# Routers of three mixtures of experts: first choice from the logits, sums by one scan, one product for all ranks, and two parts a turn for one pair

## The chip, the cores and the metric

The kernel runs on 1 core of one Trainium2 chip. The metric is the device time of one execution in microseconds (us). The core has a matmul engine (TensorE, PE in the profile; PEld is its weight load), a vector engine (VectorE, DVE), a scalar engine (ScalarE, ACT), a general engine (GpSimd, POOL) and a queue for transfers (SyncE, SP). Each engine works through its own list of instructions in order and waits for the others by semaphores.

## What is computed

Four layers stand in a row, each as half a feed-forward part, an attention, and the same feed-forward part again. The input is 4 batches of 512 tokens of 128 numbers, all float32. The feed-forward parts of layers 0 and 3 are mixtures of experts with a capacity; only their routers are changed. Cut to what matters:

```python
# layer 0 (used twice): one choice, 8 experts, capacity 320
logits = einsum('td,ed->te', tokens, gate_w)
probs = softmax(logits)
mask = one_hot(argmax(probs), 8)
ranks = cumsum(mask, axis=0) - 1.0              # over all 2048 tokens
keep = (ranks < capacity) * mask
h = relu(einsum('ecd,edh->ech', dispatch, w1) + b1)
out = einsum('ech,ehd->ecd', h, w2) + b2
ans = combined out, weighted by probs

# layer 3 (used twice): two choices, 8 experts, capacity 512
scores = softmax(xt @ wg)
gates_k, idx_k = top_k(scores, 2)
gates_k = gates_k / sum(gates_k)
m = masks of first choices of all tokens, then of second choices
loc = cumsum(m) - 1 at each token's choice      # place within the expert
valid = loc < cap
# rows are placed at (expert, loc), run through the expert, gathered back,
# weighted by gates_k * valid
```

## The kernel before

Tokens lie on the 128 partitions: a batch is 4 tiles of 128 tokens (`NT = 4`), 16 tiles in all (`TILES`).

A `Mixture` object stands for one use of such a part: `f00` and `f01` are the two of layer 0 (`k = 1`), `f30` and `f31` the two of layer 3 (`k = 2`). Its method `tokens` is the router for one batch, or for two batches together as a pair (`G = 4` or `8` tiles). It normalizes the rows (`norms`: statistics on DVE, `rs`, a power for `rstd` and sometimes `off` on POOL, then the scaling on DVE, ACT or POOL), transposes them on PE, multiplies by the gate weights (`lg`, L322), takes a softmax, and finds the first choice (`route`, and for two choices `without` and `route` again). `masks` then holds ones at the chosen expert. `pre` is a running sum of the masks over the tiles of the call and of earlier calls (`cum`), by one DVE addition for each tile (L359). The rank of a token within its expert comes from two products on PE for each choice: `before` (ones where an earlier token of the tile stands) times the mask (L368), and `ones` times `pre` (L369). From the rank DVE computes `kept`, `at`, `slot`, `keep` and the row address `to` (L372 to L385). Last, POOL copies the weights `counts` into the rows (L392) and writes each tile of rows to its place in the DRAM buffer `disp` with an indirect transfer, here called a scatter (L395): one for each tile and choice.

`experts` reads `disp` back expert by expert (`d_f`, L426, issued from SP), so it starts only when the last scatter of the mixture has landed. It runs the two matrix products, and writes rows to `res` with scatters of its own (L489); `combine` adds them to the tokens.

The routers stand in four places:

- `f00` at the start of the kernel: four batches, staggered by two turns (`skewed`).
- `f01` beside the attention of layer 0: each batch's router starts when that batch's attention output is done, so the router of batch 3 runs after the attention's end. Transposes of the next weights (`prep_l1`, L137 to L140) follow.
- `f30` at the end of a chain of feed-forward parts of layers 1 and 2. Here the batches go in two pairs, (0, 1) and (2, 3). The pairs go through the same parts, the second pair 8 turns behind the first (`whole(skewed([behind(pool, bs) for bs in pairs], 8))`). The first pair uses one call of `tokens` with `later=4`, which lets four turns pass before the scatters; the second pair uses two calls, one for each batch, 3 turns apart.
- `f31` beside the attention of layer 3, as `f01`.

A turn is one step of the Python generators, from one `yield` to the next. It sets the order in which instructions are written down. In the attentions that order is kept for PE, DVE, ACT and POOL (`manual_schedule`). In the chain with `f30` it is kept for POOL alone. Everywhere else a planner at compile time sorts each engine's list by its own estimate of when operands are ready.

The POOL list of the chain, near its end, is therefore written by hand: the norms of the first pair's router, those of batch 2, those of batch 3, the first pair's 16 scatters, the 8 of batch 2 and the 8 of batch 3.

Of the kernel before, what the change touches and what calls it, by code (L numbers as in the profile page):

```python
# [41 lines left out]
def kernel(ctx: ExitStack, tc: tile.TileContext, a: dict, out: bass.AP):  # L42
# [25 lines left out]
    for b in range(NB):  # L68
# [12 lines left out]

    before = const([P, P], "before")
    nc.gpsimd.affine_select(
        out=before, in_=ones, pattern=[[1, P]], compare_op=ALU.is_gt, fill=0.0, base=0, channel_multiplier=-1
    )
    mhalf = const([P, 2 * NT], "mhalf")
    nc.gpsimd.memset(mhalf, -0.5)
# [113 lines left out]
    def bc_mid(ap, shape):  # L201
        return ap.unsqueeze(1).to_broadcast(shape)


    def route(pool, src, g, tag, mask=None):

        mx = pool.tile([P, g], FP, name=f"mx_{tag}", tag=f"mx_{tag}")
        nc.vector.tensor_reduce(mx, src, AX.X, ALU.max)
        eq = pool.tile([P, g, E], FP, name=f"eq_{tag}", tag=f"eq_{tag}")
        nc.vector.tensor_tensor(eq, src, bc(mx, [P, g, E]), ALU.is_equal)  # L210
        nc.vector.tensor_tensor(eq, eq, bc_mid(e_rank, [P, g, E]), ALU.mult)
        first = pool.tile([P, g], FP, name=f"first_{tag}", tag=f"first_{tag}")
        nc.vector.tensor_reduce(first, eq, AX.X, ALU.max)
        if mask is None:
            mask = pool.tile([P, g, E], FP, name=f"mask_{tag}", tag=f"mask_{tag}")
        nc.vector.tensor_tensor(mask, eq, bc(first, [P, g, E]), ALU.is_equal)
        return mask, mx

    def without(pool, src, mask, g, low, tag):
        rest = pool.tile([P, g, E], FP, name=f"rest_{tag}", tag=f"rest_{tag}")  # L220
        nc.vector.scalar_tensor_tensor(rest, mask, low, src, ALU.mult, ALU.add)
        return rest

    def softmax(pool, lg, g, tag):

        mx = pool.tile([P, g], FP, name=f"smx_{tag}", tag=f"smx_{tag}")
        nc.vector.tensor_reduce(mx, lg, AX.X, ALU.max)
        pr = pool.tile([P, g, E], FP, name=f"pr_{tag}", tag=f"pr_{tag}")
        nc.vector.tensor_tensor(pr, lg, bc(mx, [P, g, E]), ALU.subtract)
        nc.scalar.activation(pr, pr, AF.Exp)  # L230
        yield
        sm = pool.tile([P, g], FP, name=f"sm_{tag}", tag=f"sm_{tag}")
        nc.vector.tensor_reduce(sm, pr, AX.X, ALU.add)
        nc.vector.reciprocal(sm, sm)
        nc.vector.tensor_tensor(pr, pr, bc(sm, [P, g, E]), ALU.mult)
        return pr

# [3 lines left out]
    class Mixture:  # L241
# [7 lines left out]
        def __init__(self, tag, cap, k):  # L249
# [32 lines left out]

        def tokens(self, bs, wT, on="vector", pool=None, fine=False, later=0):

# [7 lines left out]
            for n, b in zip(ns, bs):  # L292
                for c in range(k):
# [43 lines left out]
            counts = tile("counts", [P, k, G])  # L337
            if k == 1:
                nc.vector.tensor_scalar(counts[:, 0], best, 0.5, None, ALU.mult)
            else:  # L340
                if fine:
                    yield
                rest = without(pool, pr, masks[:, 0], G, -4.0, f"r{G}")
                _, second = route(pool, rest, G, f"r1{G}", masks[:, 1])
                total = tile("total", [P, G])
                nc.vector.tensor_tensor(total, best, second, ALU.add)
                nc.vector.reciprocal(total, total)
                nc.vector.scalar_tensor_tensor(counts[:, 0], best, 0.5, total, ALU.mult, ALU.mult)
                nc.vector.scalar_tensor_tensor(counts[:, 1], second, 0.5, total, ALU.mult, ALU.mult)
            if fine:  # L350
                yield

            pre = routing.tile([P, k, G + 1, E], FP, name=f"pre_{tag}", tag=f"pre{k}{G}")
            if self.cum is None:
                nc.vector.memset(pre[:, :, 0, :], 0.0)
            else:
                nc.vector.tensor_copy(pre[:, :, 0, :], self.cum)
            for t in range(G):
                nc.vector.tensor_tensor(pre[:, :, t + 1, :], pre[:, :, t, :], masks[:, :, t, :], ALU.add)  # L359
            self.cum = pre[:, :, G, :]  # L360
            yield
            if fine:
                yield

            ps = bank(f"rank_{tag}")[:, : k * G * E].rearrange("p (k g e) -> p k g e", k=k, e=E)
            for c in range(k):
                out = ps[:, c].rearrange("p g e -> p (g e)")
                nc.tensor.matmul(out, before, masks[:, c].rearrange("p g e -> p (g e)"), start=True, stop=False)  # L368
                nc.tensor.matmul(out, ones, pre[:, c, :G, :].rearrange("p g e -> p (g e)"), start=False, stop=True)  # L369
            yield  # L370
            kept = tile("kept", [P, k, G, E])
            nc.vector.scalar_tensor_tensor(kept, ps, float(self.cap), masks, ALU.is_lt, ALU.mult)  # L372
            at = tile("at", [P, k, G, E])
            nc.vector.tensor_tensor(at[:, 0], ps[:, 0], bc_mid(first_row[self.per], [P, G, E]), ALU.add)
            if k == 2:
                nc.vector.tensor_tensor(at[:, 1], bc_mid(last_row, [P, G, E]), ps[:, 1], ALU.subtract)
            nc.vector.tensor_tensor(at, at, kept, ALU.mult)
            slot = tile("slot", [P, k, G])
            nc.vector.tensor_reduce(slot, at, AX.X, ALU.add)
# [3 lines left out]
            nc.vector.tensor_tensor(keep, keep, spare, ALU.mult)  # L383
            to = tile("to", [P, k, G], I32)
            nc.vector.tensor_tensor(to, slot, keep, ALU.subtract)  # L385
            yield

            for _ in range(later):
                yield
            for i, n in enumerate(ns):  # L390
                for c in range(k):
                    nc.gpsimd.tensor_copy(n[:, :, 1 if c else D + 3], counts[:, c, i * NT : (i + 1) * NT])  # L392
            for c in range(k):
                for t in range(G):
# [5 lines left out]
                    )  # L400
                    if fine and t % 2:
                        yield
# [1072 lines left out]
    with tc.tile_pool(name="weights12", bufs=1) as mid:  # L1475
# [15 lines left out]
        def behind(pool, bs):  # L1491
# [70 lines left out]
```

## Time and profile before

| | |
|---|---|
| median of 3 runs | 1575.8 us (1572.78 to 1575.96) |
| profiled execution | 1557.3 us, of which the span of the profile is 1555.6 us |
| mean granted PE clock | 0.898 of full speed |
| PE busy | 1279.9 us (82%), 10651 instructions |
| DVE busy | 866.6 us (56%), 2955 instructions |
| ACT busy | 713.2 us (46%), 1487 instructions |
| POOL busy | 657.2 us (42%), 791 instructions |
| scatters of the routers (L395) | 96, 94.6 us on POOL |
| additions of the running sums (L359) | 64 on DVE |
| rank products (L368 and L369) | 88 PE records (a float32 product shows as two) |

All profile numbers come from the profiled execution and are times in us from the start of its span. In a line of a timeline the first number is the start and the second the length, then engine, source line, operation, what is written and what is read with their shapes (partitions x elements), how many such instructions were merged (x), and in brackets the idle time of the engine before it and what ended that.

### The profile page before, as it was taken

What the parts mean: (1) busy time and instruction counts of PE and PEld (TensorE: products, weight loads), DVE (VectorE), ACT (ScalarE), POOL (GpSimd) and SP (SyncE); (2) the same over time, 40 slices, a digit from 0 to 9 for tenths busy, and PEclk for the clock granted to TensorE, in tenths of its full rate; (3) what the DMA queues carried; (4) which work ended last, traced back from release to release, by engine and by line L of the source; (5) the groups of instructions that cost most, each with busy time, mean ns of one, the idle gap of its engine ahead of it and who ended that gap; (6) DMA issues with size and microseconds to landing.
All of it is one profiled execution on the core that took longest, in us unless ns stands there. A gap on an engine that the chain in (4) does not pass through costs nothing. (4 is left out here: it accounts for less than half of the span.)

```text
span 1555.6 us, 28883 instructions
## 1 busy us (share of the span) xinstructions
PE 1279.9 (82%) x10651; PEld 823.0 (53%) x10651; DVE 866.6 (56%) x2955; ACT 713.2 (46%) x1487; POOL 657.2 (42%) x791
## 2 busy tenths in 40 slices
PE   3787998995969688989989887819789999998394
PEld 3464666773755455757656666606533334333273
DVE  5325776773335366666556556615367787773343
ACT  1234876871443156768743322203336655564041
POOL 3455767772420177677510111263631224212253
PEclk9897999996989988999989878858979999999597
DMA  7520230002415375442022000014204000000233
GB/s 226 129 57 13 77 146 32 9 6 65 140 49 111 94 219 150 140 133 70 2 56 55 1 0 1 10 61 103 62 21 172 15 5 12 13 3 15 76 79 105
DMA packets 100660, 106.21 MB, mean 68 GB/s; under 512 B 9084, under 2 KB 73832, under 8 KB 100520
## 3 DMA queue, kind: packets, MB, share of 16 engines
q1 hardware_dynamic: 93864, 91.16, 20.8%
q0 software_dynamic: 6656, 13.22, 2.6%
q8 instruction: 84, 1.38, 0.4%
q14 instruction: 56, 0.46, 0.1%
HBM read 62.49 MB, written 41.85 MB: 67 GB/s over the span
## 5 line engine op out<-in xcount | busy, mean ns | idle before, releaser
L605 POOL TENSOR_SCALAR sc_a<-sc_a,top_a 128x128 f32<-128x128 f32 (+3 forms) x256 | 276.0, 1093 | 110.6 <-DVE top_a L604 75.1
L587 PE MATMUL s_a<-k_a,q_a 32*128 32x512 f32 (+3 forms) x1536 | 266.5, 548 | 17.1 <-POOL k_a L1183 13.8
L692 ACT ACTIVATE w_a<-t_a 128x512 f32<-128x512 f32 x256 | 140.4, 595 | 119.6 <-PE t_a L587 94.9
L628 PE MATMUL t_a<-ident,sc_a 128*128 128x128 f32 x1280 | 172.3, 282 | 6.2 <-DVE top_a L608 5.7
L489 POOL DMA_INDIRECT res_f<-y_f,back_f x112 | 109.8, 980 | 143.7 <-ACT y_f L488 102.3
L587 PE MATMUL t_a<-ql_a,k_a 32*128 32x512 f32 x512 | 168.8, 644 | 0.5 <-DVE low_a__12755 L672 0.2
L628 PEld LDWEIGHTS t_a<-ident,sc_a 128*128 128x128 f32 x1280 | 145.2, 144 | 36.4 <-issue 13.7
L617 ACT ACTIVATE sc_a<-sc_a,top_a 128x128 f32<-128x128 f32 (+3 forms) x256 | 134.9, 577 | 22.8 <-DVE top_a L608 22.6
L587 PEld LDWEIGHTS s_a<-k_a,q_a 32*128 32x128 f32 x1536 | 93.7, 188 | 88.1 <-issue 42.8
L637 ACT ACTIVATE w_a<-t_a 128x256 f32<-128x256 f32 (+2 forms) x192 | 94.3, 526 | 63.6 <-PE t_a L628 63.1
L395 POOL DMA_INDIRECT disp_f<-n_f,to_f x96 | 94.6, 985 | 66.7 <-issue 58.8
L501 PE MATMUL o_f<-w_l,h_f 128*128 128x128 f32 (+1 forms) x896 | 113.0, 279 | 3.8 <-DVE o_f L483 3.3
L501 PEld LDWEIGHTS o_f<-w_l,h_f 128*128 128x128 f32 (+1 forms) x896 | 103.0, 184 | 14.7 <-DVE o_f L483 6.0
L466 PE MATMUL h_f<-dT_f,w_l 128*128 128x320 f32 (+1 forms) x256 | 108.0, 560 | 2.8 <-ACT dT_f L444 2.8
L157 POOL TENSOR_SCALAR rs_f<-mv_f 128x4 f32<-128x4 f32 (+1 forms) x23 | 5.7, 248 | 230.0 <-DVE mv_f L154 229.2
L650 PE MATMUL acc_a<-w_a,vpad 128*32 128x128 f32 x2560 | 98.4, 280 | 0.6 <-DVE top_a L604 0.6
L639 ACT COPY w_a<-t_a 128x256 f32<-128x256 f32 (+2 forms) x192 | 93.7, 527 | 6.9 <-PE t_a L628 6.6
L672 DVE TENSOR_REDUCE low_a__12755<-s_a 128x1 f32<-128x512 f32 x128 | 82.1, 685 | 26.3 <-PE t_a L587 18.5
L608 DVE CUSTOM_DVE_ANT_0 sc_a<-s_a,future 128x128 f32<-128x128 f32 (+3 forms) x128 | 62.3, 487 | 56.4 <-PE s_a L587 50.3
L672 DVE TENSOR_REDUCE low_a__12753<-s_a 128x1 f32<-128x512 f32 x128 | 81.3, 683 | 20.1 <-PE t_a L587 15.0
L608 DVE CUSTOM_DVE_ANT_0 sc_a<-s_a,table 128x128 f32<-128x128 f32 (+3 forms) x128 | 62.4, 488 | 52.9 <-PE s_a L587 52.4
L488 ACT ACTIVATE y_f<-o_f,d_f 128x128 f32<-128x128 f32 (+1 forms) x112 | 38.8, 394 | 105.9 <-DVE o_f L483 105.9
(343 smaller groups left out, 2285.9 us busy)
## 6 DMA issues: line engine op xcount, KB each, us to landing
fac_a<-fac_a_sb SPq DMA_DIRECT2D x36, 256.0 KB
disp_f<-zeros_f SPq DMA_DIRECT2D x4, 2080.0 KB
d_f<-disp_f SPq DMA_DIRECT2D x32, 260.0 KB
w_l<-in_L_ffn_w_dram SPq DMA_DIRECT2D x16, 512.0 KB
cb_f<-rows_f SPq DMA_DIRECT2D x16, 512.0 KB
q_a<-fac_a SPq DMA_DIRECT2D x32, 256.0 KB
k_a<-fac_a SPq DMA_DIRECT2D x32, 256.0 KB
r_f<-res_f SPq DMA_DIRECT2D x24, 256.0 KB
```

Of the source, the lines that this page charges most:

```text
L395: nc.gpsimd.indirect_dma_start(out=self.to[c][i0 + t][:, :], out_offset=bass.IndirectOffsetOnAxis(ap=to[:, c, t : t + 1], axis=0), in_=ns[ ...
L466: nc.tensor.matmul(ps[u][:, :cap], w1[:, e, (c + u) * P : (c + u + 1) * P], dT, start=True, stop=True)
L489: nc.gpsimd.indirect_dma_start(out=self.back[e * per + s][:, :], out_offset=bass.IndirectOffsetOnAxis(ap=back[:m, s : s + 1], axis=0), in_ ...
L501: nc.tensor.matmul(po[:m, s, :], h[:, c, s * P : s * P + m], w2[:, e, c, :], start=(c == 0), stop=(c == NC - 1),)
L587: nc.tensor.matmul(ps[:, n0:n1], q[r : r + SLOT, i * P : (i + 1) * P], k[r : r + SLOT, n0:n1], start=True, stop=True)
L605: nc.gpsimd.tensor_scalar(sc, sc, top, None, ALU.subtract)
L608: nc.vector.tensor_tensor_reduce(sc, banks[r][:, :n], more, -1.0, HUGE, ALU.add, ALU.min, top)
L617: nc.scalar.activation(sc, sc, AF.Exp, bias=top, scale=-1.0)
L628: nc.tensor.transpose(ps[:, x * n + j * P : x * n + (j + 1) * P], st["sc", u, i, r0 + x][:, j * P : (j + 1) * P], ident,)
L650: nc.tensor.matmul(st["acc", u][r * SLOT : (r + 1) * SLOT, i * P : (i + 1) * P], vpads[b % 2][:, j, g * 4 + r, :], st["w", u, i, r][:, j * ...
L672: nc.vector.tensor_reduce(st["low", u][:, i, c : c + 1], ps, AX.X, ALU.max, negate=True)
L692: nc.scalar.activation(w, ps, AF.Exp)
```

## The change

The router `tokens` is rewritten in these points:

- The first choice is taken from the logits in PSUM instead of from the softmax; `softmax` as a function is gone. The exponentials are still made, for the second choice and the weights. With one choice the weight is half the reciprocal of the sum of the exponentials; with two, the best has the value 1, so the sum is `second + 1`.
- `masks`, `pre`, `kept` and `at` are laid out with the tiles innermost (`[P, k, E, G]`).
- `pre` is made by one `tensor_tensor_scan`, a multiplication by `goes_on` (zero at the first tile of each expert, else one) and an addition. It is the sum within the call and includes the tile itself; what came before is kept apart in `cum`.
- The ranks of all choices come from one accumulated product: `not_before` (the old `before` minus one) times the masks, `ones` times `cum` spread over the tiles if there is one, and `ones` times `pre`.
- `spare` and the start row of each expert minus `spare` (`ends`) are made once for each mixture; `keep` is gone, and `to` is `slot + spare`.
- `later` is gone. The first pair's call of `f30` is made with `apart=True`, which yields after every scatter, and is advanced by two parts each turn.

```diff
+    nc.vector.tensor_scalar(not_before, not_before, -1.0, None, ALU.add)
+    goes_on = {}
+    for g in (NT, 2 * NT):
+        goes_on[g] = const([P, 2 * E * g], f"goes_on{g}")
+        nc.vector.memset(goes_on[g], 1.0)
+        nc.vector.memset(goes_on[g].rearrange("p (e t) -> p e t", t=g)[:, :, 0], 0.0)
...
-    def route(pool, src, g, tag, mask=None):
+    def route(pool, src, g, tag, mask=None, mx=None):
...
+            self.spare = routing.tile([P, TILES], FP, name=f"spare_{tag}", tag=f"spare{k}", bufs=1)
+            nc.vector.tensor_scalar(self.spare, tok_id[:, :TILES], float(self.rows), None, ALU.add)
+            self.ends = routing.tile([P, k, E, TILES], FP, name=f"ends_{tag}", tag=f"ends{k}", bufs=1)
+            for c, row in enumerate((first_row[self.per], last_row)[:k]):
+                nc.vector.tensor_tensor(
+                    self.ends[:, c], bc(row, [P, E, TILES]), bc_mid(self.spare, [P, E, TILES]), ALU.subtract
+                )
...
-            spare = pool.tile([P, k, G], FP, name=f"spare_{tag}", tag=f"spare{k}{G}")
-            nc.gpsimd.tensor_scalar(
-                spare, bc_mid(tok_id[:, i0 : i0 + G], [P, k, G]), float(self.rows), None, ALU.add
-            )
...
-            pr = yield from softmax(pool, plg[:, : G * E].rearrange("p (g e) -> p g e", e=E), G, f"r{G}")
-            masks = tile("masks", [P, k, G, E])
-            _, best = route(pool, pr, G, f"r0{G}", masks[:, 0])
...
+            nc.vector.tensor_reduce(mx, lg, AX.X, ALU.max)
+            pr = tile("pr", [P, G, E])
+            nc.vector.tensor_tensor(pr, lg, bc(mx, [P, G, E]), ALU.subtract)
+            nc.scalar.activation(pr, pr, AF.Exp)
+            masks = tile("masks", [P, k, E, G])
+            by_tile = [masks[:, c].rearrange("p e g -> p g e") for c in range(k)]
+            route(pool, lg, G, f"r0{G}", by_tile[0], mx)
+            yield
+            if k == 2:
+                rest = without(pool, pr, by_tile[0], G, -4.0, f"r{G}")
+                _, second = route(pool, rest, G, f"r1{G}", by_tile[1])
                 if fine:
                     yield
...
-            for t in range(G):
-                nc.vector.tensor_tensor(pre[:, :, t + 1, :], pre[:, :, t, :], masks[:, :, t, :], ALU.add)
-            self.cum = pre[:, :, G, :]
+            nc.vector.tensor_tensor_scan(
+                pre.rearrange("p k e g -> p (k e g)"), goes_on[G][:, : k * E * G],
+                masks.rearrange("p k e g -> p (k e g)"), 0.0, ALU.mult, ALU.add,
+            )
...
-            for c in range(k):
-                out = ps[:, c].rearrange("p g e -> p (g e)")
-                nc.tensor.matmul(out, before, masks[:, c].rearrange("p g e -> p (g e)"), start=True, stop=False)
-                nc.tensor.matmul(out, ones, pre[:, c, :G, :].rearrange("p g e -> p (g e)"), start=False, stop=True)
+            nc.tensor.matmul(ps, not_before, masks.rearrange("p k e g -> p (k e g)"), start=True, stop=False)
+            if self.cum is not None:
+                nc.tensor.matmul(
+                    ps.rearrange("p (e g) -> p e g", g=G), ones,
+                    bc(self.cum.rearrange("p k e -> p (k e)"), [P, k * E, G]), start=False, stop=False,
+                )
+            nc.tensor.matmul(ps, ones, pre.rearrange("p k e g -> p (k e g)"), start=False, stop=True)
+            counts = tile("counts", [P, k, G])
+            total = tile("total", [P, G])
+            if k == 1:
+                nc.vector.tensor_reduce(total, pr, AX.X, ALU.add)
+            else:
+                nc.vector.tensor_scalar(total, second, 1.0, None, ALU.add)
+            nc.vector.reciprocal(total, total)
+            nc.vector.tensor_scalar(counts[:, 0], total, 0.5, None, ALU.mult)
+            if k == 2:
+                nc.vector.tensor_tensor(counts[:, 1], second, counts[:, 0], ALU.mult)
+            cum = routing.tile([P, k, E], FP, name=f"cum_{tag}", tag=f"cum{k}")
+            if self.cum is None:
+                nc.vector.tensor_copy(cum, pre[:, :, :, G - 1])
+            else:
+                nc.vector.tensor_tensor(cum, self.cum, pre[:, :, :, G - 1], ALU.add)
+            self.cum = cum
...
-            keep = tile("keep", [P, k, G])
-            nc.vector.tensor_reduce(keep, kept, AX.X, ALU.add)
-            nc.vector.tensor_tensor(slot, slot, spare, ALU.add)
-            nc.vector.tensor_tensor(keep, keep, spare, ALU.mult)
+            nc.vector.tensor_reduce(slot, at.rearrange("p k e g -> p k g e"), AX.X, ALU.add)
             to = tile("to", [P, k, G], I32)
-            nc.vector.tensor_tensor(to, slot, keep, ALU.subtract)
+            nc.vector.tensor_tensor(to, slot, bc_mid(self.spare[:, i0 : i0 + G], [P, k, G]), ALU.add)
             yield
-            for _ in range(later):
-                yield
...
-                    if fine and t % 2:
+                    if apart or (fine and t % 2):
                         yield
...
             if bs[0] == 0:
-                yield from f30.tokens(bs, l3["gate"], "scalar", pool, later=4)
+                parts = f30.tokens(bs, l3["gate"], "scalar", pool, apart=True)
+                while next(parts, "end") != "end" and next(parts, "end") != "end":
+                    yield
```

More of the change, by code (lines that the diff above doesn't have):

```diff
@@ L80 @@
     )
-    before = const([P, P], "before")
+    not_before = const([P, P], "not_before")
     nc.gpsimd.affine_select(
-        out=before, in_=ones, pattern=[[1, P]], compare_op=ALU.is_gt, fill=0.0, base=0, channel_multiplier=-1
+        out=not_before, in_=ones, pattern=[[1, P]], compare_op=ALU.is_gt, fill=0.0, base=0, channel_multiplier=-1
     )
+    nc.vector.tensor_scalar(not_before, not_before, -1.0, None, ALU.add)
[4 more added lines that the diff above has]
+        nc.vector.memset(goes_on[g].rearrange("p (e t) -> p e t", t=g)[:, :, 0], 0.0)
     mhalf = const([P, 2 * NT], "mhalf")
@@ L202, in bc_mid @@
         return ap.unsqueeze(1).to_broadcast(shape)
-    def route(pool, src, g, tag, mask=None):
-        mx = pool.tile([P, g], FP, name=f"mx_{tag}", tag=f"mx_{tag}")
-        nc.vector.tensor_reduce(mx, src, AX.X, ALU.max)
+    def route(pool, src, g, tag, mask=None, mx=None):
+        if mx is None:
+            mx = pool.tile([P, g], FP, name=f"mx_{tag}", tag=f"mx_{tag}")
+            nc.vector.tensor_reduce(mx, src, AX.X, ALU.max)
         eq = pool.tile([P, g, E], FP, name=f"eq_{tag}", tag=f"eq_{tag}")
@@ L222, in without @@
         return rest
[L224 to L230, printed above, removed]
-        yield
[L232 to L236, printed above, removed]
     routing = ctx.enter_context(tc.tile_pool(name="routing", bufs=2))
@@ L281, in clear, with tokens @@
             self.spread_zeros(self.res[1 : 1 + self.k * T, :])
-        def tokens(self, bs, wT, on="vector", pool=None, fine=False, later=0):
+        def tokens(self, bs, wT, on="vector", pool=None, fine=False, apart=False):
             pool = pool or routing
@@ L333, in tokens @@
             yield
-            pr = yield from softmax(pool, plg[:, : G * E].rearrange("p (g e) -> p g e", e=E), G, f"r{G}")
-            masks = tile("masks", [P, k, G, E])
-            _, best = route(pool, pr, G, f"r0{G}", masks[:, 0])
[L337 to L340, printed above, removed]
+            lg = plg[:, : G * E].rearrange("p (g e) -> p g e", e=E)
+            mx = tile("mx", [P, G])
@@ L341, in tokens @@
                 if fine:
                     yield
[L343 to L357, printed above, removed]
-            for t in range(G):
-                nc.vector.tensor_tensor(pre[:, :, t + 1, :], pre[:, :, t, :], masks[:, :, t, :], ALU.add)
-            self.cum = pre[:, :, G, :]
+            pre = routing.tile([P, k, E, G], FP, name=f"pre_{tag}", tag=f"pre{k}{G}")
@@ L361, in tokens @@
+            nc.vector.tensor_tensor_scan(
+                pre.rearrange("p k e g -> p (k e g)"),
+                goes_on[G][:, : k * E * G],
+                masks.rearrange("p k e g -> p (k e g)"),
+                0.0, ALU.mult, ALU.add,
+            )
             yield
@@ L363, in tokens @@
                 yield
[L365 to L369 removed]
+            ps = bank(f"rank_{tag}")[:, : k * E * G]
@@ new lines, in tokens @@
+            nc.tensor.matmul(ps, not_before, masks.rearrange("p k e g -> p (k e g)"), start=True, stop=False)
[5 more added lines that the diff above has]
+            nc.tensor.matmul(ps, ones, pre.rearrange("p k e g -> p (k e g)"), start=False, stop=True)
+            ps = ps.rearrange("p (k e g) -> p k e g", k=k, e=E)
@@ L370, in tokens @@
+            cum = routing.tile([P, k, E], FP, name=f"cum_{tag}", tag=f"cum{k}")
[4 more added lines that the diff above has]
+            self.cum = cum
             yield
-            kept = tile("kept", [P, k, G, E])
+            kept = tile("kept", [P, k, E, G])
             nc.vector.scalar_tensor_tensor(kept, ps, float(self.cap), masks, ALU.is_lt, ALU.mult)
-            at = tile("at", [P, k, G, E])
@@ L374, in tokens @@
-            nc.vector.tensor_tensor(at[:, 0], ps[:, 0], bc_mid(first_row[self.per], [P, G, E]), ALU.add)
+            at = tile("at", [P, k, E, G])
+            nc.vector.tensor_tensor(at[:, 0], ps[:, 0], self.ends[:, 0, :, i0 : i0 + G], ALU.add)
             if k == 2:
-                nc.vector.tensor_tensor(at[:, 1], bc_mid(last_row, [P, G, E]), ps[:, 1], ALU.subtract)
+                nc.vector.tensor_tensor(at[:, 1], self.ends[:, 1, :, i0 : i0 + G], ps[:, 1], ALU.subtract)
             nc.vector.tensor_tensor(at, at, kept, ALU.mult)
@@ L378, in tokens @@
             slot = tile("slot", [P, k, G])
-            nc.vector.tensor_reduce(slot, at, AX.X, ALU.add)
-            keep = tile("keep", [P, k, G])
-            nc.vector.tensor_reduce(keep, kept, AX.X, ALU.add)
-            nc.vector.tensor_tensor(slot, slot, spare, ALU.add)
-            nc.vector.tensor_tensor(keep, keep, spare, ALU.mult)
+            nc.vector.tensor_reduce(slot, at.rearrange("p k e g -> p k g e"), AX.X, ALU.add)
             to = tile("to", [P, k, G], I32)
-            nc.vector.tensor_tensor(to, slot, keep, ALU.subtract)
+            nc.vector.tensor_tensor(to, slot, bc_mid(self.spare[:, i0 : i0 + G], [P, k, G]), ALU.add)
@@ L386, in tokens @@
             yield
-            for _ in range(later):
-                yield
             for i, n in enumerate(ns):
```

## Prediction

> **What bounds the kernel now.** I read the table of windows first. TensorE (PE) is 82% busy over the span, and from 272 to 350 and from 1167 to 1400 us it is at 98 to 100%: there the attentions set the time and a router beside them costs little. Four gaps are different. In each a router or its scatters is the last thing before `experts`, and PE has nothing to do.
>
> Windows (length, then busy us of PE, PE weight loads, DVE, ACT, POOL, then PE clock, DMA share, GB/s):
> ```profile
> 1003.00:1012.00 9.00, 5.14 (x20) 4.22 (x20) 4.34 (x34) 2.46 (x6) 7.02 (x11) 0.50 0.13 44
> 1012.00:1044.00 32.00, 4.00 (x16) 3.25 (x16) 4.11 (x29) 0.27 (x1) 24.66 (x32) 0.50 0.15 50
> 1450.00:1469.00 19.00, 0.74 (x4) 0.64 (x4) 2.08 (x12) 0.00 (x0) 7.83 (x8) 0.50 0.39 106
> ```
> For 32 us only POOL works, and it does nothing but row scatters. Timeline of that gap (start, us, engine, line, operation):
> ```profile
> 993.53 0.17 DVE L385 TENSOR_TENSOR to_f<-slot_f,keep_f 128x16 int32<-128x16 f32 x1
> ...
> 1001.36 1.04 POOL L158 TENSOR_TENSOR rstd_f<-rs_f,mhalf 128x4 f32<-128x4 f32 x1
> ...
> 1003.65 1.13 POOL L395 DMA_INDIRECT disp_f<-n_f,to_f  x1 [0.15 <-POOL n_f L392]
> 1005.09 0.96 POOL L395 DMA_INDIRECT disp_f<-n_f,to_f  x1 [0.31 <-issue]
> ...
> 1043.88 0.96 POOL L395 DMA_INDIRECT disp_f<-n_f,to_f  x1 [0.31 <-issue]
> ```
> The first pair's addresses (`to_f`, 16 columns) are ready at 993.7, but its scatters start at 1003.65, behind the norms of batch 3: POOL's order is written by hand here, and `later=4` puts them there. Then 32 scatters follow 1.265 us apart (0.96 and 0.30 of issue) to 1044.84, and the experts' reads wait for the last one.
>
> The other three gaps are router chains on DVE. The last one:
> ```profile
> 1443.70 0.19 DVE L227 TENSOR_REDUCE smx_r<-lg_f 128x4 f32<-128x32 f32 x1 [7.01 <-PE lg_f L322]
> ...
> 1444.41 0.19 DVE L233 TENSOR_REDUCE sm_r<-pr_r 128x4 f32<-128x32 f32 x1 [0.29 <-ACT pr_r L230]
> 1444.64 0.18 DVE L234 RECIPROCAL sm_r<-sm_r 128x4 f32<-128x4 f32 x1
> ...
> 1448.18 0.84 DVE L359 TENSOR_TENSOR pre_f<-pre_f,masks_f 128x16 f32<-128x16 f32 x4
> ...
> 1450.39 0.23 DVE L372 SCALAR_TENSOR_TENSOR kept_f<-rank_f,masks_f 128x64 f32<-128x64 f32 x1 [1.37 <-PE rank_f L369]
> ...
> 1451.90 0.17 DVE L385 TENSOR_TENSOR to_f<-slot_f,keep_f 128x8 int32<-128x8 f32 x1 [0.22 <-DVE keep_f L383]
> 1452.83 1.11 POOL L395 DMA_INDIRECT disp_f<-n_f,to_f  x1 [4.46 <-issue]
> ```
> Each dependent DVE step takes 0.22 us whatever little it does; the scatter starts 0.76 after `to_f`. The same chain ends the second mixture (367.32 to 374.93, scatter 375.69) and paces the first (`to_f` of batch 1 at 38.76, then 12 scatters without a gap from 39.53 to 54.70, reads issued at 57.18).
>
> [...]128x4 costs 0.16, 128x32 0.19, 128x512 0.69. [...]128x512 scan (L1323) 1.216 against 0.69 for a tensor_tensor. [...]The windows show 0.50 in the gaps and 1.00 from 1062 on[...].[...]
>
> **The change, part by part.**
>
> *1. Shorter router, exposed at the end of `f31`.* Gone from the way to `to`: the wait for exp, sum, reciprocal, multiply and second maximum of the first choice; the copy and four adds become one scan; `keep`'s reduce and multiply and one more add; four rank products become three, of which only the last waits for the scan. New chain from 1443.70: maximum, subtract, equal, rank, maximum, mask: 6 x 0.223 = 1.34; `rest` to second mask: 6 x 0.223 = 1.34; scan of 64: between the 0.22 of a 128x64 tensor_tensor and 0.42; from the 1.216 at twice 1.05 ns an element I take 0.3; last product 0.65 (a pair at this clock); `total`, reciprocal, counts and `cum`, 5 small ops queued before `kept`, reach 0.3 beyond that product; kept, two `at`, product, slot, `to`: 1.3. Sum 5.3, `to` at 1449.0 against 1452.07: **3.0 saved** (2 to 3.6). The 8 scatters and the reads follow unchanged.
>
> *2. The same at the end of `f01`.* One choice: 6 steps 1.34, scan 0.22, product 0.65, counts 0.2, five steps 1.05: 3.5 instead of 7.6 (367.32 to 374.93). DVE and PE also do weight transposes and copies of `prep_l1` here (1.1 us of copies lay inside the old chain), so I take **3.2** (1.5 to 4). Beyond 3.8 SP would be late next: its loads before the reads end at 378.42, the reads were issued at 382.18.
>
> *3. `f00`.* Batch 1's logits are done at 30.04, its `to` came at 38.76 because four routers share DVE in the planner's order (it stood 1.6 us for batch 2's logits). The bare chain is 3.5, and PE's next logits block is 1.9 us, so `to` at 34 to 36.5: 2.3 to 4.8 earlier, and the 12 scatters with it. After them comes a read that would meet the table's loads still landing until 56. I take **3.0** (0 to 5).
>
> *4. New constants.* `not_before` 0.3, four memsets of 0.07 to 0.17 and strided ones alike, `spare` and `ends` 0.2 to 0.5 per mixture: some 1.2 us of DVE before the first norms, some of which delay `tok_id` (9.98), which POOL waits for. In return POOL loses two `spare` (0.3 each with its gap) ahead of `rstd` at 12.71. Net 0, bounds -0.6 and +1.0. The later mixtures' constants hide behind PE, which is busy; without that cover, 1.2 us each.
>
> *5. Routers beside the attentions.* About 8 DVE ops fewer each (1.3 us) and no DVE wait on ACT's exp; three batches of `f01` get a carry product instead (two more PE records, 0.3 us), those of `f31` one or two products fewer. PE is the bound: net **-0.5** (-3 to +1.5).
>
> *6. The pair's choice, two parts a turn, in `f30`.* POOL's hand order becomes: the pair's scatters 1-10, norms of batch 2, scatters 11-16, norms of batch 3, then their scatters. What waits behind a late `to` is thus batch 2's norm, its router and all after it. When is `to` ready? Logits are done at 976.5, as now. 13 DVE steps at 0.256 (128x64) are 3.3, about 8 gate products of 0.68 that the planner slips between them now add 4.4, the rank pairs 0.7, six last steps 1.6: 986.5, first scatter about **987**; bounds 985 and 991. From that start T0: ten scatters 12.8, ids and norm of batch 2 2.4, six scatters 7.6, ids and norm of batch 3 2.4. Batch 2's `to` comes 9.3 to 10.4 after its norm (norm, transposes and logits 3.8 to 4.9 as at 996.9 to 1000.7, then part 1's 5.4), so its scatters start about T0 + 26, last 10.1, and with copies of 0.6 batch 3's start at T0 + 36.5; end T0 + 46.5 to 48.5. Break-even against 1044.84 is T0 = 997.3. With 987: **10 saved** (5 to 13). Batch 3's router is late next, just hidden by batch 2's scatters. SP issues no other load between 960 and 1046.7, so no queue is passed.
>
> Sum: 3.0 + 3.2 + 3.0 + 0 + 0.5 + 10 = 19.7. The profiled execution took 1557.3 (span 1555.6, 1.7 around it), 1.2% under the median of 1575.8; against its own time the sum gives 1537.6. The gaps hold little PE work, so I subtract the same microseconds from the median: 1575.8 - 19.7 = **1556**.
>
> **Rivals.**
> - *A: the pair's scatters hardly start earlier.* If DVE keeps the gate products ahead of the router, T0 is 993 to 995 and part 6 gives 3: 12.7 in all, 1563. For it: five products lay between the last router steps at 990 to 993.5. Against: the router now comes before them in program order.
> - *B: the first two tails are hidden.* `f00`'s reads meet the table traffic and `f01`'s chain is broken by `prep_l1`'s copies: parts 2 and 3 give 1 together, 14.5 in all, 1561.
> - *C: slower, through POOL.* The pair's scatters now run beside DVE's 128x512 products and ahead of the norms of batches 2 and 3. If each were stretched by d, all that follows shifts by 16d. It cancels part 6 at d = 0.63 and the whole sum at 1.23, that is 2.5 us a scatter; at d = 1.6 the time is 1582. Against: beside DVE's 128x512 score operations at 300 to 304 four scatters stood 1.27 apart[...].
> - *D: it doesn't shorten.* The carry product adds PE records, and the shifted turns let an in-order engine wait for the scan: a draw if that costs 0.5 at each of 12 turns (two of each of six routers) and A and B hold too: 7.5 - 6 = 1.5 left, 1574.
>
> **How the numbers follow.** Forecast 0.60, A 0.14, B 0.12, D 0.05, C 0.09. Low end: the upper bounds of all parts together, 3.6 + 4 + 5 + 0.6 + 3 + 13 = 29.2, give 1546.6. High end: A and B together leave 7.5: 1568. The range 1546 to 1568 leaves out most of C and D and little else. A difference of 0.2% (3.2 us) is about what can be told here. Faster 0.87, same 0.04, slower 0.09.
>
> **What would show it.** Right: the first pair's scatter near 987, ten scatters before batch 2's `rstd`, the last `f30` scatter near 1034 on the old clock; `smx` to `to` of the last batch 5.3 us in `f31` and 4 in `f01`; `f00`'s last scatter near 51. Part 6 is wrong if POOL stands idle between scatters 16 and 17 for over 2 us or if spacing exceeds 1.3. The whole is wrong if the gaps shrink but the attention stretches grow by as much.

## The result and the profile after

| | before | after |
|---|---|---|
| median of 6 runs each | 1573.99 us (1572.36 to 1575.96) | 1560.91 us (1557.24 to 1562.56) |
| ratio after / before | | 0.9912, 95% interval 0.9897 to 0.9927 |
| profiled execution, span | 1557.3 us, 1555.6 us | 1560.92 us, 1559.2 us |
| busy PE, DVE, POOL | 1279.9, 866.6, 657.2 us | 1292.6, 852.1, 654.3 us |

The change saves 13.1 us where 19.7 were forecast: faster, inside the range, two thirds of the sum. The two spans can't be subtracted from each other. Run again, the kernel before took 1558.0 on another chip, in agreement with its first profile (experiment e1), and 1571.6 on a third: this program differs by 1% from chip to chip, and the two first profiles seem to be from two sorts. There is no profile of the kernel before on a chip as slow as that of the result, so the 13.1 us can't be divided among the stages there. Below, stages are compared, and where possible profiles of one sort.

The windows of the gaps in the profile after (columns as in the prediction):

```profile
984.50:1003.60 19.10, 18.55 (x111) 13.10 (x108) 11.75 (x25) 0.00 (x0) 10.19 (x12) 0.86 0.11 36
1003.60:1022.40 18.80, 10.76 (x74) 9.72 (x72) 6.60 (x40) 4.93 (x12) 10.06 (x18) 0.76 0.07 21
1022.40:1043.40 21.00, 3.50 (x14) 2.82 (x14) 4.00 (x25) 0.27 (x1) 16.46 (x20) 0.50 0.15 48
```

The last window is the old gap, 21 us where it was 32. But in the first PE is full of the second pair's products, which now end at 1008.4 and ended at 996.7, and in the second POOL is busy for 10.06 of 18.8. The timeline of POOL says where it stood:

```profile
984.79 1.13 POOL L406 DMA_INDIRECT disp_f<-n_f,to_f  x1 [3.01 <-DVE to_f L399]
...
996.32 0.96 POOL L406 DMA_INDIRECT disp_f<-n_f,to_f  x1 [0.30 <-issue]
997.31 0.44 POOL L297 TENSOR_SCALAR n_f<-tok_id 128x4 f32<-128x4 f32 x2
1003.64 0.22 POOL L164 TENSOR_SCALAR rs_f<-mv_f 128x4 f32<-128x4 f32 x1 [5.89 <-DVE mv_f L161]
...
1022.43 1.12 POOL L406 DMA_INDIRECT disp_f<-n_f,to_f  x1 [6.47 <-DVE masks_f L224]
...
1042.07 0.95 POOL L406 DMA_INDIRECT disp_f<-n_f,to_f  x1 [0.31 <-issue]
```

The first scatter comes at 984.8 (forecast 987), ten scatters go out without a gap, and then POOL waits twice: 5.89 us for batch 2's statistics and 6.47 us for batch 2's addresses. (The second bracket names the DVE step that ended last before the scatter, which is one of batch 3's; batch 2's `to` ended at 1021.58.) Without the two waits the last scatter would have ended at 1043.0 - 12.4 = 1030.7, near the forecast 1034.

The first wait comes from the order of the lists of DVE and PE. In the profile before, the gate products of the second pair come first, and its batch 2 is done at 989.3:

```profile
977.57 1.29 DVE L1301 TENSOR_TENSOR gb_f<-gate_f,nT_f 128x512 f32<-128x512 f32 x2 [0.57 <-PE gate_f L1298]
...
989.32 0.68 DVE L1290 SCALAR_TENSOR_TENSOR x<-y_f,x 128x512 f32<-128x512 f32 x1
```

In the profile after, the router's last step comes first, then the first eight gate products, and batch 2 (`x`) follows ten us later than before:

```profile
983.80 0.17 DVE L399 TENSOR_TENSOR to_f<-slot_f,spare_f 128x16 int32<-128x16 f32 x1
984.47 4.88 DVE L1312 TENSOR_TENSOR gb_f<-gate_f,nT_f 128x512 f32<-128x512 f32 x8 [0.50 <-PE gate_f L1309]
...
999.29 0.69 DVE L1301 SCALAR_TENSOR_TENSOR x<-y_f,x 128x512 f32<-128x512 f32 x1 [3.79 <-PE gate_f L1309]
```

PE shows where these steps of DVE come from. In its list the gate products now stand behind the router's rank products, and PE is idle for 4.03 us until the router's chain has come that far:

```profile
981.24 0.77 PE L363 MATMUL rank_f<-masks_f,not_before 128*128 128x128 f32 x2 [4.03 <-DVE counts_f L381]
...
982.36 3.80 PE L1309 MATMUL gate_f<-gT_f,row 32*128 32x512 f32 x16
```

In the profile before they start at 976.41:

```profile
976.41 2.00 PE L1298 MATMUL gate_f<-gT_f,row 32*128 32x512 f32 x16
```

Part of the 4.03 us is a wait of DVE's for the exponentials, which the second choice needs. ACT makes them late, behind a copy of the transposed gates (`gT`) and a load of its function table:

```profile
977.91 1.28 ACT L338 ACT_TABLE_LOAD   x1
...
979.49 0.27 DVE L229 SCALAR_TENSOR_TENSOR rest_r<-masks_f,pr_f 128x64 f32<-128x64 f32 x1 [1.75 <-ACT pr_f L338]
```

In the profile before the same load starts at 976.30, and DVE works on gate products in the meantime.

Of the ten us, more than four belong to the slower chip. In e9, the same kernel on a faster chip, batch 2's `x` starts 18.5 us after the router's first DVE step (12.8 in the profile before, 23.0 in the profile after). POOL's first wait is 1.57 us there, and the second is as long as here:

```profile
998.96 0.22 POOL L164 TENSOR_SCALAR rs_f<-mv_f 128x4 f32<-128x4 f32 x1 [1.57 <-DVE mv_f L161]
...
1017.68 1.12 POOL L406 DMA_INDIRECT disp_f<-n_f,to_f  x1 [6.46 <-DVE masks_f L224]
```

The difference lies in the third group of gate products, eight records. It lasts 4.4 us in the profile after, with pauses, though the clock granted there is 1.00, and 1.14 in e9, which is what eight of these records take at a granted clock of 1.00 in the profile after (at 989.93). The profile after:

```profile
995.10 2.24 PE L1309 MATMUL gate_f<-gT_f,row 32*128 32x512 f32 x5
997.65 1.82 PE L1309 MATMUL gate_f<-gT_f,row 32*128 32x512 f32 x3 [0.30 <-issue]
```

And e9:

```profile
994.37 1.14 PE L1309 MATMUL gate_f<-gT_f,row 32*128 32x512 f32 x8
```

In e5, the kernel after on a slower chip once more, the group has a pause too (seven records in 2.51 us, 0.29 idle, then the eighth). Why PE is slow at this place there is open.

The second wait is PE's order. PE's timeline after:

```profile
1016.29 1.63 PE L187 MATMUL T_f<-ident,n_f 128*128 128x128 f32 x4 [5.68 <-ACT n_f L174]
1017.72 0.53 PE L363 MATMUL rank_f<-masks_f,not_before 128*128 128x64 f32 x2
...
1018.47 0.63 PE L369 MATMUL rank_f<-pre_f,ones 128*128 128x64 f32 x2
```

Batch 2's scan is done at 1013.7, but its rank products stand in PE's list behind the transposes of batch 3, which wait for batch 3's norm, which stands on POOL behind scatters 11 to 16.

The short chains came out as follows. Last batch of `f31`, DVE:

```profile
1448.75 0.19 DVE L334 TENSOR_REDUCE mx_f<-lg_f 128x4 f32<-128x32 f32 x1 [7.01 <-PE lg_f L320]
...
1451.44 0.29 DVE L352 TENSOR_TENSOR_SCAN pre_f<-goes_on,masks_f 128x64 f32<-128x64 f32 x1
...
1454.18 0.17 DVE L399 TENSOR_TENSOR to_f<-slot_f,spare_f 128x8 int32<-128x8 f32 x1
```

5.60 us from the first step to the end of `to`, where it was 8.36. In `f01` it is 5.92, where it was 7.61 and 3.5 was forecast: PE and DVE put weight transposes and their copies between the steps, as these two lines of that chain show.

```profile
374.83 0.17 DVE L134 COPY gate1T<-ps_gate1T 128x8 f32<-128x8 f32 x1 [1.08 <-PE ps_gate1T L147]
...
377.05 0.69 DVE L134 COPY wu1T<-ps_wu1T 128x512 f32<-128x512 f32 x1 [1.03 <-PE ps_wu1T L147]
```

### The profile page after: what moved, and what is told of

It reads as the page before. It is cut to its first block, busy times and chain, and to the rows that moved or that the text cites. A ratio compares the mean times of both kernels' runs of the same rounds, so it can differ in the third digit from the quotient of the medians.

```text
span 1559.2 us, 28753 instructions
## 1 busy us (share of the span) xinstructions
PE 1292.6 (83%) x10645; PEld 828.5 (53%) x10645; DVE 852.1 (55%) x2832; ACT 713.4 (46%) x1487; POOL 654.3 (42%) x776
## 5 line engine op out<-in xcount | busy, mean ns | idle before, releaser
L598 PE MATMUL s_a<-k_a,q_a 32*128 32x512 f32 (+3 forms) x1536 | 264.4, 544 | 17.4 <-POOL k_a L1194 13.3
L683 DVE TENSOR_REDUCE low_a__12648<-s_a 128x1 f32<-128x512 f32 x128 | 82.0, 684 | 26.6 <-PE t_a L598 19.3
```

What stands on the lines that cost most here:

```text
L598: nc.tensor.matmul(ps[:, n0:n1], q[r : r + SLOT, i * P : (i + 1) * P], k[r : r + SLOT, n0:n1], start=True, stop=True)
L683: nc.vector.tensor_reduce(st["low", u][:, i, c : c + 1], ps, AX.X, ALU.max, negate=True)
```

## The experiments

All were timed beside the kernel before. The first four and the last four ran on chips where that takes 1558.0 and 1557.4 (below: the faster chips), the middle four where it takes 1571.6 (a slower chip, like the one of the result).

**e1, the kernel before once more** (no edit).

> The kernel before, unchanged, profiled once more: its first profile (span 1555.6) is some 17 us under its timed executions (1572 to 1576). If the first profile was a lucky execution, this one has a span near 1572, and the difference lies in a few places that can be named. If being profiled makes this kernel shorter, the span is near 1556 again while the time stays near 1574.

Median 1557.76, ratio 0.9997 (0.9988 to 1.0007), span 1557.2. Neither expectation: the time itself is 1558 here, profiled or not. So the 17 us of the first profile are most likely a matter of the chip (which chip that was is not known), not of luck in one execution. Stage by stage the two profiles differ by up to 3 us each way.

**e2, the routers alone.**

```diff
-                parts = f30.tokens(bs, l3["gate"], "scalar", pool, apart=True)
-                while next(parts, "end") != "end" and next(parts, "end") != "end":
-                    yield
+                yield from f30.tokens(bs, l3["gate"], "scalar", pool, later=4)
...
+            for _ in range(later):
+                yield
```

> The new routers with the old turns (one part a turn, four turns before the scatters, no yield between them). Theory 1 (the pair's early scatters gain nothing: 5.9 us of POOL waiting for batch 2's statistics and 6.5 us waiting for batch 2's addresses eat them up): as fast as the kernel after, 1558 to 1564. Rival 2 (the turns bring the forecast 10 us, the routers only the rest): 1568 to 1573.

1543.82, ratio 0.9911 (0.9898 to 0.9924): 13.9 us saved without the turns. The forecast had 9.7 for the routers. It was expected as a time of the slower chip; as a ratio it is what theory 1 said, and rival 2 (1568 to 1573 of 1574 is 0.996 to 0.999) falls.

**e3, the turns alone.** The kernel before, with the pair's two parts a turn and a yield after each scatter.

```diff
-                yield from f30.tokens(bs, l3["gate"], "scalar", pool, later=4)
+                parts = f30.tokens(bs, l3["gate"], "scalar", pool, apart=True)
+                while next(parts, "end") != "end" and next(parts, "end") != "end":
+                    yield
...
-                    if fine and t % 2:
+                    if apart or (fine and t % 2):
```

> The old routers with the new turns of the pair (two parts a turn, a yield after each scatter). Theory 1: no gain, 1572 to 1577; POOL waits some 6 us for batch 2's statistics between the tenth and the eleventh scatter. Rival 2: 1563 to 1567, with less than 2 us of such waiting.

1560.66, ratio 1.0020 (1.0011 to 1.0029): 3 us slower. The early start is there (first scatter at 992.8), but the last one starts at 1048.8, later than in e1 (1045.5). The large wait was not where I put it: 1.1 us for batch 2's statistics, 9.3 us for batch 2's addresses.

**e4, the router one part a turn, the scatters two a turn.** The kernel after, with

```diff
                 parts = f30.tokens(bs, l3["gate"], "scalar", pool, apart=True)
+                for _ in range(8):
+                    next(parts)
+                    yield
                 while next(parts, "end") != "end" and next(parts, "end") != "end":
```

> The kernel after, but the pair's router goes one part a turn up to its addresses, and only its scatters go two a turn: POOL's order is then two scatters, norm of batch 2, six scatters, norm of batch 3, eight scatters. Theory 1 (the two-parts-a-turn router takes DVE and PE from batch 2's gate products): first scatter near 992, seven later than after, but no wait over 2 us from there on, so the last scatter of the stage ends 44 to 48 after the first, near 1038 on the clock of the profile after (1043.0); time 5 to 8 under the kernel after, about 1554. Rival 2 (the early start is what counts): the last scatter is late by the seven us of the start, and the time is 3 to 7 over the kernel after.

1542.02, ratio 0.9892 (0.9877 to 0.9907). POOL's timeline of e4:

```profile
990.05 1.13 POOL L406 DMA_INDIRECT disp_f<-n_f,to_f  x1 [8.34 <-DVE gb_f L1312]
...
992.99 0.22 POOL L164 TENSOR_SCALAR rs_f<-mv_f 128x4 f32<-128x4 f32 x1
...
1003.07 0.22 POOL L164 TENSOR_SCALAR rs_f<-mv_f 128x4 f32<-128x4 f32 x1
...
1035.09 0.96 POOL L406 DMA_INDIRECT disp_f<-n_f,to_f  x1 [0.31 <-issue]
```

The stage does what theory 1 said: both norms start without a wait, no scatter behind them waits for more than 0.31 us, and 46.0 us after the first scatter the last one has ended, though the first starts five us later than in the kernel after. Starting the router's work later lets the scatters end earlier. The time was to be 5 to 8 under the kernel after; against that kernel's ratio on a faster chip (0.9886, e9) there is no difference that the intervals allow.

**e5, the kernel after again, and e6, e7, e8, the new router in one mixture alone.** In the last three, old and new `tokens` stand side by side and one mixture takes the new; all keep the old turns.

```diff
+        def tokens(self, *args, **kwargs):
+            how = self.tokens_new if self.tag in ('f31',) else self.tokens_old
+            return how(*args, **kwargs)
```

> The kernel after, unchanged, beside the kernel before on the same chip. Theory 1 (the turns bring nothing): ratio to before 0.990 to 0.993, the same as with the new routers alone (0.9911), and the pair's stage is as long as before, 77 to 80 us from the pair's norm to the end of the last scatter. If ratio and profile on the first chip were a matter of that chip, the ratio is below 0.988.

0.9932 (0.9914 to 0.9950), and the stage is 77.2 us long: as theory 1 expected.

> The kernel before with the new router in the last mixture (f31) alone. The sum of the forecast has 3.0 for its end and 0.5 shared among routers beside attentions: ratio 0.998. If routers beside the attention also save PE time there (2.9 us between 1160 and 1400 in the profiles of routers-only and before on one chip), the ratio is 0.996.

0.9937 (0.9921 to 0.9954), 9.8 us: most of what the change brings on this sort of chip, and more than either value. The end of `f31` takes 33.8 us in its profile (36.6 in e7 and e8, with the old router there), the attention of layer 3 takes 315.5 (321.6 and 318.6). It takes 319.5 and 318.4 with the whole change on such chips, so in this stage the whole change keeps less than its last part alone; why is open.

> The kernel before with the new router in the second mixture (f01) alone. The forecast has 3.2 for its end: ratio 0.998. Rival (what the router saves is lost to the weight transposes and the reads' queue): 0.9995 to 1.0005.

> The kernel before with the new router in f30 alone and the old turns. The forecast counted nothing for this without the turns: ratio 0.9995 to 1.0005. Theory 1b (fewer DVE steps between the gate products let batch 2's tokens finish earlier[...]: the pair's stage was 75.4 us with the new routers against 80.5 and 77.5 in two executions before): 0.9965 to 0.998.

1.0015 (1.0006 to 1.0024) and 1.0022 (1.0008 to 1.0037). These two can't be read as times: the first expert of `f00` starts at 66 instead of 61, 5 us that belong to neither theory. SP's list is why. In both runs it has the first read of the dispatched rows ahead of two loads of the position table (`rev`, for the attention of layer 0), as e10 below shows for the kernel after. The lines of e7:

```profile
56.29 0.36 SPq L586 DMA_DIRECT2D d_f<-disp_f  x1
56.75 0.95 SPq L1103 DMA_DIRECT2D rev<-tab_rows  x2
```

PE, which has the table's products ahead of the first expert, waits 10.43 us for these loads (9.60 in e8). The kernel before and e6 have all these loads ahead of the reads. What moved SP's order is not known (e6 lacks the constant `goes_on` for eight tiles, which e7 and e8 have). The first scatter is 2 us later than in e6 (30.5 against 28.5), because DVE's list has batch 1's first step, which waits 1.65 us for its logits, ahead of batch 0's last ones; the last scatter is only 0.9 later. In their profiles the stages themselves can be read: the end of `f01` 25.0 us against 26.4 and 26.3 in e6 and e8, the stage of `f30` 75.2 against 77.2 in e6. So the shorter router without the turns saves 2.0 us in `f30`, less than the smaller gain of e8's theory 1b (0.998, 3.1 us).

**e9, the kernel after on a faster chip, and e10, the table first.** In e10 SP's list is kept as written:

```diff
-        whole(made)
-        prep_l0_attn()
-        f00.experts(l0["w"])
+        with tc.manual_schedule(engines={mybir.EngineType.SP}):
+            whole(made)
+            prep_l0_attn()
+            f00.experts(l0["w"])
```

> The kernel after once more, on the chip of the next three, for their differences. Ratio to before 0.990 to 0.995.

> The kernel after, with SP's order kept as written from the position table's loads to the first mixture's experts, so that the table's loads and the weights' loads are issued before the first read of dispatched rows. Theory 1 (the 6 us that f00's scatters gained are lost because two of the table's loads are queued on SP behind the first read, which waits for the scatters, and PE's list has the table's products ahead of the first expert): the experts of f00 start 4 to 6 us earlier than the 61 of after, and the time is 3 to 6 under the kernel after. Rival 4 (the DMA engines are full, the order doesn't matter): 60 to 62 again, and no difference.

e9: 1539.97, 0.9886 (0.9872 to 0.9901). e10: 1539.17, 0.9878 (0.9864 to 0.9893). PE's timeline of e9 in front of `f00`'s experts:

```profile
55.18 3.84 PE L959 MATMUL turned<-rev,flip 128*128 128x512 f32 x4 [8.76 <-DMA rev<-tab_rows]
...
60.05 0.91 PE L453 MATMUL dT_f<-ident,d_f 128*128 128x128 f32 x3
61.59 2.42 PE L477 MATMUL h_f<-dT_f,w_l 128*128 128x320 f32 x8 [0.64 <-ACT dT_f L455]
```

SP's list in e9:

```profile
50.07 0.36 SPq L437 DMA_DIRECT2D d_f<-disp_f  x1
50.53 0.94 SPq L954 DMA_DIRECT2D rev<-tab_rows  x2
```

PE in e10:

```profile
54.67 0.95 PE L453 MATMUL dT_f<-ident,d_f 128*128 128x128 f32 x3 [3.18 <-DMA d_f<-disp_f]
56.26 4.63 PE L477 MATMUL h_f<-dT_f,w_l 128*128 128x320 f32 x8 [0.64 <-ACT dT_f L455]
```

And SP in e10:

```profile
40.42 2.87 SPq L954 DMA_DIRECT2D rev<-tab_rows  x3
...
51.86 1.44 SPq L437 DMA_DIRECT2D d_f<-disp_f  x3
```

In e9 the scatters of `f00` are early (the last at 47.6), but two of the table's loads stand on SP behind the first read, which waits for those scatters, and PE's list has the table's products ahead of the first expert. With the loads issued first, the expert starts 5.4 us earlier, as theory 1 said; rival 4 falls. Half of it is given back at once: the same eight records now take 4.63 us instead of 2.42. They take 4.63 in the profile before too, where the clock granted to them is 0.50. From 65 us on e10 is 2.5 us ahead, which its time (0.8 less) neither confirms nor excludes.

**e11, table first and e4's turns.** Both edits above.

> Table first, and the pair's router one part a turn with its scatters two a turn. Theory 1: the pair's stage (first rstd to the end of the last scatter) is 70 to 71 us where after has 77.2, so 5 to 8 under table first alone, 9 to 13 under after. Rival 2 (nothing but noise in the stage): the same as table first.

1539.31, 0.9887 (0.9873 to 0.9901). The stage is 70.4 us long, as expected (e10: 72.9, not 77.2), and the profiled span is 3.7 under e10's; the medians are equal. No version is shown to beat the kernel after.

**e12, one chain of rank products for each choice.**

```diff
-            nc.tensor.matmul(ps, not_before, masks.rearrange("p k e g -> p (k e g)"), start=True, stop=False)
...
+            for c in range(k):
+                part = ps[:, c].rearrange("p e g -> p (e g)")
+                nc.tensor.matmul(
+                    part, not_before, masks[:, c].rearrange("p e g -> p (e g)"), start=True, stop=False
+                )
+                if self.cum is not None:
+                    nc.tensor.matmul(ps[:, c], ones, bc(self.cum[:, c], [P, E, G]), start=False, stop=False)
+                nc.tensor.matmul(part, ones, pre[:, c].rearrange("p e g -> p (e g)"), start=False, stop=True)
```

> The kernel after, with the ranks made by one chain of products for each choice, as before, where after has one for all. Theory 1 (beside the attention of layer 3, where PE is never idle, each rank block costs PE what it lasts: 1.0 us before and 0.5 to 0.75 after, with what it breaks up around it): the attention of layer 3 longer by 2 to 3, the end of f31 by 0.5, the time 2.5 to 4 over the kernel after. Rival (the products are hidden): within 1 us of after.

1549.51, 0.9944 (0.9928 to 0.9959): 9.5 over e9, more than expected. The attention of layer 3 is 1.6 longer and the end of `f31` 0.8, in the direction of theory 1, and the "hidden" rival falls. But 3.7 us are in the stage of `f30`, which I had not thought of: PE's list now starts on the first choice's product, the planner puts eight gate products between the router's later steps, and `to` comes 22.7 instead of 18.1 us after the pair's `rstd`. The spans of the two profiled executions differ by 7.2, of which these stages are 6.1; the rest is not assigned.

Why a rank block (the rank products of one batch) costs time beside the attention is seen where PE is never idle. e1, batch 0 of `f31`, four products (two records each), then the attention goes on after 1.00 us:

```profile
1276.02 0.41 PE L368 MATMUL rank_f<-masks_f,before 128*128 128x32 f32 x2
...
1276.71 0.39 PE L369 MATMUL rank_f<-pre_f,ones 128*128 128x32 f32 x2
1277.02 0.69 PE L587 MATMUL s_a<-k_a,q_a 32*128 32x512 f32 x1
```

The same block in e2, after 0.49:

```profile
1266.28 0.33 PE L363 MATMUL rank_f<-masks_f,not_before 128*128 128x64 f32 x2
1266.45 0.39 PE L369 MATMUL rank_f<-pre_f,ones 128*128 128x64 f32 x2
1266.77 0.69 PE L600 MATMUL s_a<-k_a,q_a 32*128 32x512 f32 x1
```

Around each of the first two batches' blocks e2 gains 1.3 to 1.4 us on e1: 0.5 by the block itself, the rest by the attention's products around it, which are ordered otherwise there.

The stages in us, from the profiles (first expert: the start of ACT's first copy of `dT`; f30: from the start of the pair's `rstd` to the end of the last scatter; attention of layer 3: from the start of the last scatter of `f30`'s experts to the end of the attention's last projection; end: from there to the first expert):

| | before, first | e1 before | e2 routers | e4 | e9 after | after, first (slower chip) | e5 after (slower chip) |
|---|---|---|---|---|---|---|---|
| start to first expert of f00 | 61.0 | 60.8 | 60.7 | 61.6 | 61.1 | 61.3 | 60.9 |
| end of f01 | 26.9 | 26.6 | 25.1 | 25.1 | 25.0 | 24.8 | 25.3 |
| f30 | 77.2 | 80.2 | 75.1 | 70.4 | 72.9 | 77.3 | 77.2 |
| attention of layer 3 | 314.3 | 313.5 | 310.5 | 310.7 | 310.6 | 319.5 | 318.4 |
| end of f31 | 36.9 | 36.6 | 34.1 | 33.8 | 34.1 | 34.2 | 34.2 |

## Why the prediction was right, and where its sum was wrong

- **Faster, by a sum of short chains: right in kind, too large.** 13.1 us against 19.7 on the chip of the result, 17.8 (1.14% of 1557.4, e9) on a faster one. The parts missed in both directions, and that their sum stayed in the range is in part luck.
- **1, end of `f31`: right.** 5.60 us for the chain against a forecast of 5.3, 2.8 saved against 3.0. The scan of 64 took 0.29 (estimate 0.3).
- **2, end of `f01`: half.** 1.7 saved against 3.2. I counted bare steps, though the copies of `prep_l1` in the old chain were in my own text; they stay, and the chain now waits for them.
- **3, `f00`: the scatters earlier than I said, the gain nothing.** The last scatter starts 6.2 us earlier (53.74 to 47.54). Of this 3.7 come from batch 1's logits, which are done at 26.4 and not at 30.04, where I had left them; the router behind them gives 2.4, inside my 2.3 to 4.8. The first expert is no earlier. It is rival B's place, but not its mechanism: not traffic, but two loads behind a waiting read in SP's order (e10).
- **4, constants: no cost seen.** The kernel after has all of them, and its first scatter is 4.4 us earlier than before (24.78 against 29.16). Their cost was not measured alone; the 5 us of e7 and e8 are SP's order.
- **5, beside the attentions: mis-sized.** 0.5 forecast; the attention of layer 3 is 3.4 shorter on the faster chips (313.9, mean of the two before, to 310.6), that of layer 0 no shorter.
- **6, two parts a turn: the step that failed.** "With 987: 10 saved". T0 came out (984.8), but by luck: the sum for it has 4.4 us of gate products between the router's steps, and none stands there; a wait of 1.75 us for the exponentials does, which the sum put at nothing. The sum from T0 on took batch 2's norm as ready whenever POOL came to it, and its router as 9.3 to 10.4 us. Neither holds: POOL waits 1.57 us for the statistics on the faster chip and 5.89 on the slower, and `to` starts 17.4 us after `rstd`. The profile before had 16.4 for the same way (995.21 to 1011.56). On the slower chip the stage keeps its 77.2 us; on the faster one it shrinks to 72.9, of which 2.1 come from the shorter router (e2: 75.1, e1 left aside, whose first 16 gate records took 3.80 us as at half clock). So by stage the turns save 2.2 on the faster chips and lose 2.0 on the slower (e8: 75.2); by time they save at most some 4 (0.9886 against 0.9911, the intervals touch).

What POOL waits for after the tenth scatter is batch 2's tokens. They are late because the router goes ahead of the gate products on DVE and PE: these start at 982.4 where they started at 976.4. On the slower chip the slow third group adds over four us.

PE's clock has a part that stays open. The first 16 gate records take 3.80 us instead of 2.00: the clock granted in the profile after is 0.50 from 965.8 to 986.3, where the profile before has 1.00 from 974.4 on. In both profiles every stretch at half clock, but for the last, which the end cuts off, is a multiple of 3.41 us (3.41 to 58.0); the one here is 20.5 us. But it starts 11 us ahead of the pause of 4.03, and the logits ahead of the pause ran at half clock already (1.88 and 1.72 us for 8 records each, where 16 took 1.85 in the profile before). In e5 and e9, with a pause of 4.02, the 16 gate records take 3.80 as well, and in e4, without one, 2.00. But in e1, with the old order and without such a pause, they take 3.80 too, and PE is busy without a gap from 973.8 to their end at 980.6. So it is not shown that the pause costs clock, nor that shorter gaps cost none, which was my estimate.

The second wait is a number to remember: in e2, e4, e9 and the first profile after alike, batch 2's `to` starts 7.3 us after batch 3's `rstd`, though its own `rstd` is 13.5 us ahead of it in e2 and 17.4 to 17.5 in the others. In the profile after:

```profile
1014.07 1.04 POOL L165 TENSOR_TENSOR rstd_f<-rs_f,mhalf 128x4 f32<-128x4 f32 x1
...
1021.41 0.17 DVE L399 TENSOR_TENSOR to_f<-slot_f,spare_f 128x8 int32<-128x8 f32 x1
```

In the kernel before it is 10.2 after batch 3's. The order of PE that does this could be read in the profile before: there too batch 3's transposes (1003.6) stand ahead of batch 2's last rank products (1009.6). I took the length of a chain and didn't ask what stands in front of it.

The signal that I named for part 6 being wrong, POOL idle for over 2 us between scatters 16 and 17, showed it: 6.47. Of the rivals, A fell (the scatters are early; between 990 and 993.5 the profile before has four gate products, not five), and C is not it (the scatters are 1.265 apart). D comes nearest, an in-order engine that waits for the router, but it had 0.5 us at each of twelve turns. What came were a few long waits that take the place of the one removed, on other engines than POOL.

The stages of e9 against the mean of the two profiles before give -0.2 + 1.8 + 5.8 + 3.4 + 2.7 = 13.5 (the 5.8 of `f30` is 4.3 against the first profile alone). The spans differ by 13.4, so the other stages, up to 2.1 either way, cancel out. The 17.8 is a matter of medians: the profiled execution of e9 was the slowest of its four, 1544.7 against a median of 1539.97.

## What to carry to other kernels

When work is moved forward in a list, follow each engine that it uses, not only the one whose gap it is to fill: here the same turns that fed POOL early took DVE and PE from the next batch, whose `x` came ten us later. A chain's length is its steps plus whatever stands in front of one of them in an in-order list (batch 2's `to` starts 17.4 us after its `rstd`, not 9.3 to 10.4), so look up that neighbour for each engine change in the chain. Early work whose consumer waited for something else, or for a queue that waited for it, brought nothing here: `f00`'s last scatter starts 6.2 us earlier, its first expert no earlier. Where a planner sorts the lists, look also at those that the edit doesn't touch: SP's order changed in the kernel after, and the gain of `f00` was lost to it.

## What was not expected of the hardware

- The same program differs by chip: the kernel after has spans of 1559.2 and 1562.0 on two executions and 1543.0 on a third. In the attention of layer 3 the slower ones take 8 to 9 us more; part of it, in the profile after, is PE standing still once for 2.1 us (for `w_a` of ACT) and once for 1.0 (for `low_a` of DVE), waits that the profile before does not have. Why is open.
- Five microseconds at the first expert became 2.5 behind it, as eight records took 4.63 us where they had taken 2.42 (e10).
- PE can be busy without a pause and stay at half clock, by the length of its records: in e1 from 973.8 to 980.6 (14 logit records in 3.13 us, 16 gate records in 3.80), while in the profile before the clock granted is 0.50 up to 974.4 and 1.00 from there on, after 3.4 us in which PE was busy for 3.31.
